# Importance of the tokens in a fused attention and top-k attention kernel: through a row in DRAM instead of through TensorE and ScalarE

## The chip, the core and the metric

The kernel runs on one core of a Trainium2 chip. A core has five engines with instruction queues of their own: TensorE (PE in the profile; its weight loads are PEld), VectorE (DVE), ScalarE (ACT), GpSimd (POOL) and SyncE (SP). Each works through its queue in order. DMAs are issued by SP, ScalarE and GpSimd and are carried out by 16 DMA engines that all of them share. SBUF is the on-chip memory with 128 partitions, PSUM the memory that TensorE writes, in 8 banks.

The metric is the device time of one execution in microseconds, the median of the runs; one more execution is profiled.

## The reference

Two layers work on a batch of 8 images with 512 channels and 32 x 32 = 1024 tokens, in float32. Layer 0 is a GroupNorm and a full self-attention of 8 heads with a residual. Layer 1, which the change is in, is this (cut to what matters):

```python
q, kk, v = (einsum('oc,bcn->bon', w, xf) for w in (wq, wk, wv))
importance = nan_to_num(sum(xf * xf, axis=1), nan=0.0, posinf=0.0, neginf=0.0)
_, idx = top_k(importance, 256)                   # per image
q_sel, k_sel, v_sel = q[:, :, idx], kk[:, :, idx], v[:, :, idx]      # as tokens x channels
q_sel, k_sel = layer_norm(q_sel, ln_w, ln_b), layer_norm(k_sel, ln_w, ln_b)
attn = softmax(clip(q_sel @ k_sel.T * 512 ** -0.5, -80, 80))
out = v with the columns idx replaced by (attn @ v_sel).T
return x + wo @ out
```

The importance of a token is the sum of squares of its 512 channels. The 256 most important tokens of each image attend to each other; all other tokens keep their value.

## The kernel before

**Layer 0** takes most of the time (up to about 1960 us). Its last steps already do the first part of layer 1 for image 0 (b0), `spread_row` and `imp` of b0 included (`importance`, lines 1094 to 1099). What follows about the order of steps is for b1 to b7.

**Layer 1** is cut into small steps, each a function of an image `b` and an index. They follow each other in an order written out by hand: the strings `BATCH` (lines 60 to 72) and `END` (lines 73 to 104). A word is a step's name and index; each `-` behind it means one image earlier, each `+` one image later. `BATCH` is run through once for each image while the steady part lasts, so that in one pass the early steps of one image (`row`, `square`, `finite`, `spread`, `imp`, `count`, `vo`), the middle steps of the image before (`selt`, `qk`, `stats`, `norm`, `score`) and the last steps of the images before that (`att`, `attput`, `fetch`, `back`, `add`) are woven together. `END` does the same for the last images. Inside `tc.manual_schedule` (lines 594 to 605) this order is the order of every engine's queue, SP's too.

For one image the steps that matter here are:

- `row` (lines 245 to 248): TensorE transposes 128 tokens into a PSUM bank; `square` (line 253): ScalarE squares and sums each token's channels, so that `norm[p, j]` is the importance of token `128 j + p`. `keep_row` and `put` copy the tokens and store them to DRAM.
- `finite` (lines 261 to 267): VectorE replaces infinities and NaN and leaves the result in `col`, 128 partitions x 8 columns.
- `spread_row` (lines 269 to 275): TensorE transposes each column of `col`, repeated 128 times, with the identity. The result is that the 1024 importances stand side by side in every partition of two PSUM banks (`pi`). Each call makes four transposes and fills one bank.
- `imp` (lines 277 to 279): ScalarE copies the two banks to SBUF, into `imp`, 128 x 1024. There is one buffer of it.
- `count` (lines 281 to 304): for each of 8 groups of 128 tokens, VectorE compares every token's importance (a scalar of its partition, from `col`) with all 1024 in `imp` and sums up how many are larger, or equal and ahead of it. `place` (lines 329 to 333) adds the counts: this is the token's rank. `pick`, `holder` and `who` make the list of the 256 chosen tokens from the ranks, and `getx` gathers them from DRAM.
- `selt` and `qk`: the chosen tokens are transposed and multiplied with the weights. `stats`, `root` and `norm` (lines 410 to 437) are the LayerNorm on VectorE, with a square root on ScalarE; they end in `rows`. `normt` (line 444) transposes `rows` on TensorE, in two groups of eight matmuls, the first for q, the second for k. `score`, `clip`, `exp`, `probt`, `att` and `attk` are the attention.
- `attput` (line 528): SP stores the attended tokens to DRAM (`sa`). `fetch` (line 534): GpSimd gathers them into their places among the values `V`, 8 gathers for an image. `back` (line 550): TensorE transposes `V` back to channels x tokens (`po`). `add` (line 558): VectorE adds the residual, and SP stores the result and loads a later residual (`residual`, line 544).

PSUM banks are handed out in turn, 8 of them: a new tile waits until the tile eight before it has been read. The weights of layer 1 are loaded once; the images come in with `load_x1` (line 215).

In a pass of `BATCH`, `finite` of image t stands between `back` and `add` steps of earlier images and the `selt` and `qk` steps of image t-1. VectorE's queue after `finite` is: one `add`, five of the eight counts of image t, the LayerNorm of image t-1, then the other counts between later steps. `attput` of image t-2 comes soon after `finite` in the order, ahead of a pair of output store and residual load for each `add`.

Of the kernel before, what the change touches and what calls it, by code (L numbers as in the profile page):

```python
# [9 lines left out]
F32 = mybir.dt.float32  # L10
# [8 lines left out]
P = 128  # L19
B = 8  # L20
C = 512
N = 1024
# [35 lines left out]


BATCH = """  # L60
vkeep6- square1 inv-- put4 put2 holder- add3--- keep1 square2 back4--- att0-- att1-- who-
row6 put1 row0 add4--- row7 keep0 back7--- square0 row3 keep6 attk0-- put0 square3 vo0 row5
vput7- square6 getx- vput4- attk1-- keep3 square7 square5 add7--- vput5- back6--- keep7
finite vo1 attput-- add6--- vput0- vkeep0 keep5 selt1- selt0- spread1 spread0 fetch1-- imp1 imp0
count2 fetch0-- put6 count5 vo3 count7 vkeep1 selk1- selk0- qk1- count6 count3 qk0-
fetch5-- qk2- vput6- vput3- stats0- stats1- vput2- qk3- root0- stats2- root2- fetch2-- norm0-
vkeep3 put5 norm2- vput1- root1- vo4 vkeep4 stats3- fetch3-- norm1- vo2 root3- back0--
fetch6-- fetch4-- norm3- fetch7-- normt1- normt0- count4 vkeep2 add0-- put3 put7 back5--
normt2- normt3- scale2- scale3- row4+ add5-- back1-- scale1- count0 back2-- vo5 scale0-
count1 square4+ keep4+ place score0- score1- clip- back3-- vo6 vkeep5 pick0 add1-- exp- vo7  # L70
getv- add2-- pick1 row2+ probt- vkeep7 row1+ probk- keep2+
"""
END = """
vput2-- put4- vkeep6-- row3- add3---- square2- holder-- att1--- back4---- row0- who-- inv---
put2- row7- square1- keep1- attk1--- att0--- getx-- square3- keep3- keep0- keep7- put1- put3-
put7- row5- back6---- attk0--- row6- square7- back7---- square6- add4---- square0- square5-
keep5- keep6- put0- vput5-- vo1- put5- selt1-- finite- vkeep1- spread1- add6---- add7----
selk1-- selt0-- spread0- imp1- imp0- attput--- count1- vo0- row6 row2 vput7-- selk0-- count6-
keep6 keep2 row1 square2 count0- count2- vput6-- count7- row0 count3- vkeep0- square1 keep1
put1 vput1-- qk0-- row7 qk1-- put6- square0 put2 stats1-- qk3-- stats0-- count5- put6 keep7  # L80
square6 vo7- put7 root1-- vput1- fetch5--- row4 root0-- norm0-- qk2-- keep0 stats3--
fetch3--- count4- vo6- place- square4 vkeep7- keep4 norm1-- square7 root3-- stats2-- row3
vput0- vkeep6- vo4- normt1-- root2-- norm3-- normt0-- vput0-- row5 keep3 fetch1--- vput4--
vput3-- norm2-- vkeep4- scale1-- normt2-- put3 normt3-- scale0-- fetch2--- pick1- scale2--
square5 square3 keep5 put5 vo2- fetch0--- pick0- holder- finite spread0 scale3-- put4 vkeep2-
imp0 getv-- fetch6--- spread1 who- imp1 score0-- back2--- count4 score1-- fetch7--- count2
clip-- exp-- count3 vput2- back0--- count7 getx- vput4- count6 put0 add0--- vo3- count0
fetch4--- probt-- vkeep3- probk-- inv-- add2--- att0-- att1-- attk1-- attk0-- selt1- selt0-
selk1- selk0- attput-- count5 fetch6-- count1 qk3- place stats3- pick0 back3--- back4---
vput6- add4--- root3- pick1 back1--- qk2- fetch4-- qk0- fetch0-- norm3- add3--- fetch2--  # L90
vput7- back7--- stats2- stats0- holder fetch3-- fetch1-- qk1- who vput3- add7--- root0-
root2- add1--- back5--- norm2- getx add5--- back6--- vo5- normt3- stats1- norm0- fetch7--
root1- fetch5-- norm1- normt2- vkeep5- add6--- normt0- normt1- back2-- scale0- scale3-
scale2- back5-- back7-- vput5- add2-- back1-- add1-- selt1 back6-- back3-- scale1- add7--
add5-- score0- add6-- back0-- selt0 score1- selk1 add3-- clip- selk0 qk2 exp- stats2 back4--
qk1 probt- probk- stats1 getv- add0-- qk0 qk3 att1- root2 root1 norm2 norm1 stats0 inv-
stats3 add4-- root0 attk1- vo1 att0- root3 norm3 vkeep1 norm0 attk0- normt3 normt2 normt0
attput- scale3 normt1 fetch5- scale0 scale1 fetch7- fetch6- vo0 vkeep0 scale2 score1 fetch1-
score0 clip vsel1 fetch4- vo3 exp vselk1 vsel0 vselk0 probt fetch0- probk fetch2- vkeep3 vo6
att1 inv fetch3- att0 vo7 vkeep6 vo2 back0- attk1 back2- back4- attk0 vkeep7 back3- attput  # L100
vkeep2 add3- add0- back5- vo4 fetch7 fetch3 vo5 vkeep4 add2- back1- back7- fetch2 back6-
fetch0 fetch1 add4- add1- fetch6 add7- add5- back2 back4 add4 add6- back0 back6 fetch4 vkeep5
add0 fetch5 back3 back7 add2 back1 add6 back5 add3 add7 add1 add5
"""


# [12 lines left out]
def attention_then_topk_attention(  # L119
# [55 lines left out]
    x_dram = [dram.tile([N, C], F32, tag=f"sx{b}", name=f"sx{b}") for b in range(B)]  # L175
    v_dram = [dram.tile([N, C], F32, tag=f"sv{b}", name=f"sv{b}") for b in range(B)]
    a_dram = [dram.tile([TOP, C], F32, tag=f"sa{b}", name=f"sa{b}") for b in range(B)]


    before = const.tile([P, P], F32, tag="before", name="before")  # L180
# [45 lines left out]
    tiles, pools, x1, w = {}, {"r1": keep_pool}, {}, {}  # L226
# [50 lines left out]
    def imp(b, j):  # L277
        t = get("rp", ("imp", b), [P, N], "imp", 1)
        nc.scalar.copy(t[:, ts(j, HALF)], tiles["pi", b, j])

    def count(b, j):

        cnt = get("r1", ("count", b), [P, 3, NB], "count", 2)
        imps = tiles["imp", b]
        mine = tiles["col", b][:, j : j + 1]
        lo, hi = j * P, (j + 1) * P
        junk = tiles.get("junk")
        if junk is None:
            junk = pools["rp"].tile([P, N], F32, tag="junk", name=f"junk_{b}_{j}", bufs=1)
        if lo:  # L290
            nc.vector.tensor_scalar(  # L291
                junk[:, :lo], imps[:, :lo], mine, None, ALU.is_ge, ALU.add,
                accum_out=cnt[:, 0, j : j + 1],
            )
# [260 lines left out]
    def add(b, i):  # L555
# [52 lines left out]
    def layer0():  # L608
        with ExitStack() as st:
# [668 lines left out]
```

## Time and profile before

| | us |
|---|---|
| median of 3 runs | 2457.42 (2457.2 to 2458.29) |
| the profiled execution | 2457.09 |
| its span, from the first to the last instruction | 2455.4 |
| TensorE busy in the span | 2411.7 (98%) |
| VectorE busy | 1950.4 (79%) |
| ScalarE busy | 1405.2 (57%) |
| GpSimd busy | 1162.5 (47%) |
| `b_pi<-ident,col`, line 273, TensorE, x56 | 0.27 each, pipelined |
| `imp<-b_pi`, line 279, ScalarE, x14 | 0.60 each |
| counts, line 297, VectorE, x64 | 0.34 to 1.28 each, by width |
| counts, line 291, VectorE, x56 | 0.34 to 1.15 each, by width |

An instruction of the profile is named by its line, its engine, its operation and `out<-in`, with buffer numbers left out. A matmul's duration overlaps the next one's, so a busy TensorE isn't a TensorE at its peak. In a row of the order of time the first number is the start in us from the span's start, the second the duration; brackets behind a row give the engine's idle time before it and what ended it. `SPq` rows are DMAs being issued by SP. The share of the DMA engines is the mean over the core's 16.

### The profile page before, as it was taken

To read this page: it belongs to the slowest core of one execution; us is meant where nothing else is said; L and a number is where in the kernel's file an instruction comes from. 1 tells how busy PE (TensorE), PEld (TensorE's weight loads), DVE (VectorE), ACT (ScalarE), POOL (GpSimd) and SP (SyncE) were. 2 spreads that over 40 slices of the span, in tenths; PEclk is the share of its full clock that TensorE was granted. 3 is DMA by queue.
4 is the path that set the end of the run, shared out by engine and by line. 5 is a ranking of instruction groups with operands and counts; after the bars stand their busy time and mean duration, and the time that the engine had idled before them with its cause. 6 is when DMAs were issued, how large, how long until landed. Compare 5 with 4: busy or idle time off the path is not lost. (4 is left out here: it accounts for less than half of the span.)

```text
span 2455.4 us, 32009 instructions
## 1 busy us (share of the span) xinstructions
PE 2411.7 (98%) x11724; PEld 969.0 (39%) x11724; DVE 1950.4 (79%) x2946; ACT 1405.2 (57%) x1828; POOL 1162.5 (47%) x557
## 2 busy tenths in 40 slices
PE   7999999999999999999999999999999999999998
PEld 3333333333333333333333333333333345555554
DVE  4899988988898889888988897889877466666683
ACT  2767656665676567666665675567656523333421
POOL 0556645655556456645655555556545401111122
PEclk9999999999999999999999999999999999999999
DMA  3001112111201120112011211111112444567553
GB/s 138 31 31 61 35 57 84 34 44 60 86 32 44 61 78 26 48 57 78 27 56 53 74 44 44 61 40 65 57 56 99 151 140 155 207 204 241 190 192 107
DMA packets 108252, 205.55 MB, mean 84 GB/s; under 512 B 19114, under 2 KB 19370, under 8 KB 108096
## 3 DMA queue, kind: packets, MB, share of 16 engines
q1 hardware_dynamic: 82432, 159.95, 19.4%
q10 hardware_dynamic: 18144, 31.48, 3.4%
q0 software_dynamic: 7520, 12.09, 1.7%
q8 instruction: 92, 1.51, 0.2%
q14 instruction: 64, 0.52, 0.1%
HBM read 146.29 MB, written 69.73 MB: 88 GB/s over the span
## 5 line engine op out<-in xcount | busy, mean ns | idle before, releaser
L1012 POOL TENSOR_TENSOR es<-es,e 128x1024 f32<-128x1024 f32 x384 | 913.4, 2379 | 59.1 <-ACT e L1007 30.9
L953 ACT COPY e<-sc 128x1024 f32<-128x1024 f32 x512 | 510.1, 1009 | 379.5 <-DVE high L959 266.8
L1004 DVE TENSOR_TENSOR e<-e,ns 128x1024 f32<-128x1024 f32 x512 | 594.8, 1215 | 1.2 <-ACT ns L1000 1.1
L1007 ACT ACTIVATE e<-e 128x1024 f32<-128x1024 f32 x512 | 532.0, 1056 | 49.9 <-DVE e L1004 36.4
L1012 POOL TENSOR_TENSOR es<-e,e 128x1024 f32<-128x1024 f32 x64 | 152.6, 2384 | 816.2 <-ACT e L1007 807.1
L945 PE MATMUL sc<-q,k 64*128 64x512 f32 x2048 | 511.0, 617 | 7.2 <-ACT e L953 6.5
L959 DVE TENSOR_TENSOR high<-sc,high 128x1024 f32<-128x1024 f32 x384 | 468.4, 1220 | 43.3 <-PE sc L945 24.5
L1020 PE MATMUL av<-e,v 128*64 128x512 f32 x2048 | 476.0, 596 | 4.5 <-DVE o L1062 4.3
L744 PE MATMUL g<-x,wqkv 128*64 128x512 f32 x1984 | 453.0, 598 | 0.0
L945 PEld LDWEIGHTS sc<-q,k 64*128 64x128 f32 x2048 | 175.7, 186 | 310.6 <-issue 214.4
L1020 PEld LDWEIGHTS av<-e,v 128*64 128x64 f32 x2048 | 144.1, 137 | 303.4 <-issue 285.0
L744 PEld LDWEIGHTS g<-x,wqkv 128*64 128x64 f32 x1984 | 131.4, 136 | 305.9 <-issue 291.3
L744 PE MATMUL g<-wqkv,x 128*64 128x256 f32 x1920 | 220.8, 383 | 0.0
L744 PE MATMUL g<-o,wp 128*64 128x512 f32 x912 | 207.0, 595 | 0.0
L1049 DVE RECIPROCAL rs<-rs 128x256 f32<-128x256 f32 x64 | 112.1, 1752 | 95.8 <-ACT rs L1043 95.8
L744 PEld LDWEIGHTS g<-wqkv,x 128*64 128x64 f32 x1920 | 132.7, 137 | 107.0 <-issue 36.6
L534 POOL DMA_INDIRECT V<-sa,at x64 | 64.0, 1000 | 155.1 <-DMA sa<-att 87.5
L959 DVE TENSOR_TENSOR high<-sc,e 128x1024 f32<-128x1024 f32 x64 | 77.6, 1213 | 52.3 <-ACT e L953 51.7
L744 PEld LDWEIGHTS g<-o,wp 128*64 128x64 f32 x912 | 64.4, 137 | 134.1 <-issue 117.9
L309 PE MATMUL b_pv<-w,x 128*128 128x512 f32 x256 | 115.4, 598 | 0.0
L405 PE MATMUL b_pp<-w,selT 128*128 128x512 f32 x256 | 112.3, 593 | 0.7 <-ACT selT L396 0.7
L363 POOL DMA_INDIRECT sel<-sx,who x16 | 16.1, 1008 | 194.7 <-PE b_po L550 48.4
(177 smaller groups left out, 1990.6 us busy)
## 6 DMA issues: line engine op xcount, KB each, us to landing
nb<-negd SPq DMA_DIRECT2D x128, 256.0 KB, 3.6
x<-in_x_dram SPq DMA_DIRECT2D x32, 512.0 KB, 5.9
ri<-rsd SPq DMA_DIRECT2D x128, 128.0 KB, 2.8
sx<-xT ACTq DMA_DIRECT2D x64, 256.0 KB, 3.2
xr<-in_x_dram SPq DMA_DIRECT2D x58, 256.0 KB, 3.4
x1d<-xr SPq DMA_DIRECT2D x58, 256.0 KB, 4.0
sv<-V ACTq DMA_DIRECT2D x56, 256.0 KB, 3.1
y<-x1d SPq DMA_DIRECT2D x48, 256.0 KB, 4.8
```

Source lines behind the costliest of these rows:

```text
L309: nc.tensor.matmul(pv, x1[b][k][:, ts(j, P)], w["vo"][:, k, :], start=(k == 0), stop=(k == CT - 1),)
L405: nc.tensor.matmul(pp, tiles["selT", b][:, k, ts(rb, P)], w["qk"[which]][:, k, :], start=(k == 0), stop=(k == CT - 1),)
L534: nc.gpsimd.indirect_dma_start(tiles["V", b][:, j, :], None, a_dram[b][:, :], bass.IndirectOffsetOnAxis(ap=tiles["at", b][:, j : j + 1], a ...
L744: nc.tensor.matmul(out[r, :], wide_[:, r], moving, start=(k == 0), stop=(k == CT - 1),)
L945: nc.tensor.matmul(sc[:, hh, :], ks[p][r, ts(j, P)], qs[p][r, ts(hf, HALF)], start=True, stop=True,)
L953: nc.scalar.copy(raw[t, j], banks["s", t, j])
L959: nc.vector.tensor_tensor(high[t], banks["s", t, j], raw[t, 0] if j == 1 else high[t], ALU.max)
L1004: nc.vector.tensor_tensor(raw[t, j], raw[t, j], high[t], ALU.add)
L1007: nc.scalar.activation(raw[t, j], raw[t, j], AF.Exp, scale=QK_SCALE)
L1012: nc.gpsimd.tensor_add(sums[t], raw[t, 0] if j == 1 else sums[t], raw[t, j])
L1020: nc.tensor.matmul(avs[t][HD * hh : HD * hh + HD, :], vs[p // 2][:, j, (p % 2) * P + HD * hh : (p % 2) * P + HD * hh + HD], e[:, hh, :], s ...
L1049: nc.vector.reciprocal(rs[:, : HALF // 2], rs[:, : HALF // 2])
```

## The change

For b1 to b7 the two steps `spread` (twice) and `imp` (twice) are replaced by `nput` and `nget`. `nput` is a DMA issued by SP that stores `col` to a row of 1024 floats in DRAM, `n_dram[b]`, in the order of the tokens: element `[p, a]` of `col` goes to position `128 a + p`. `nget` is a DMA issued by SP that loads this row into each of the 128 partitions of `imp`; it waits for `nput`. Both stand directly behind `finite` in `BATCH` and `END`, and so in SP's queue ahead of `attput` of an earlier image in most passes. The counts read the same `imp` as before. For b0 the end of layer 0 still uses `spread_row` and `imp`. The words of `BATCH` and `END` after this point are the same in the same order, but for the missing ones and for `count1` of b6 in `END`, which moves from ahead of `vo0-` to behind `keep2`, so that VectorE makes count 6 of b6 ahead of count 1.

```diff
 BATCH = """
...
-finite vo1 attput-- add6--- vput0- vkeep0 keep5 selt1- selt0- spread1 spread0 fetch1-- imp1 imp0
-count2 fetch0-- put6 count5 vo3 count7 ...
+... finite nput
+nget vo1 attput-- add6--- vput0- vkeep0 keep5 selt1- selt0- fetch1-- fetch0-- put6 vo3 count2
+count5 count7 ...
...
 END = """
...
-keep5- keep6- put0- vput5-- vo1- put5- selt1-- finite- vkeep1- spread1- add6---- add7----
-selk1-- selt0-- spread0- imp1- imp0- attput--- count1- vo0- row6 row2 vput7-- selk0-- count6-
+keep5- keep6- put0- vput5-- vo1- put5- selt1-- finite- nput- nget- vkeep1- add6---- add7----
+selk1-- selt0-- attput--- vo0- row6 row2 vput7-- selk0-- count6- keep6 keep2 count1- row1
...
-square5 square3 keep5 put5 vo2- fetch0--- pick0- holder- finite spread0 scale3-- put4 vkeep2-
-imp0 getv-- fetch6--- spread1 who- imp1 score0-- back2--- count4 score1-- fetch7--- count2
+pick0- holder- finite nput nget scale3-- put4 vkeep2- getv-- fetch6--- who- score0-- back2---
+count4 score1-- fetch7--- count2 ...
...
+    n_dram = [dram.tile([N], F32, tag=f"sn{b}", name=f"sn{b}") for b in range(B)]
...
+    def nput(b, _):
+        nc.sync.dma_start(n_dram[b].rearrange("(a p) -> p a", p=P), tiles["col", b])
+
+    def nget(b, _):
+
+        nc.sync.dma_start(
+            get("rp", ("imp", b), [P, N], "imp", 1), n_dram[b].unsqueeze(0).to_broadcast([P, N])
+        )
...
     STEPS1 = {
...
-        "spread": spread_row, "imp": imp, "count": count, "vo": vo, "vkeep": vkeep,
+        "nput": nput, "nget": nget, "count": count, "vo": vo, "vkeep": vkeep,
...
-    EARLY = {"row", "square", "keep", "put", "finite", "spread", "imp", "count", "vo", "vkeep", "vput"}
+    EARLY = {"row", "square", "keep", "put", "finite", "nput", "nget", "count", "vo", "vkeep", "vput"}
```

More of the change, by code (lines that the diff above doesn't have):

```diff
@@ L60 @@
 BATCH = """
-vkeep6- square1 inv-- put4 put2 holder- add3--- keep1 square2 back4--- att0-- att1-- who-
-row6 put1 row0 add4--- row7 keep0 back7--- square0 row3 keep6 attk0-- put0 square3 vo0 row5
-vput7- square6 getx- vput4- attk1-- keep3 square7 square5 add7--- vput5- back6--- keep7
-finite vo1 attput-- add6--- vput0- vkeep0 keep5 selt1- selt0- spread1 spread0 fetch1-- imp1 imp0
[L65 to L71, printed above, removed]
+vkeep6- square1 inv-- put4 put2 holder- add3--- keep1 square2 back4--- att0-- att1-- who- row6
+put1 row0 add4--- row7 keep0 back7--- square0 row3 keep6 attk0-- put0 square3 vo0 row5 vput7-
+square6 getx- vput4- attk1-- keep3 square7 square5 add7--- vput5- back6--- keep7 finite nput
+nget vo1 attput-- add6--- vput0- vkeep0 keep5 selt1- selt0- fetch1-- fetch0-- put6 vo3 count2
+count5 count7 vkeep1 selk1- selk0- qk1- count6 count3 qk0- fetch5-- qk2- vput6- vput3- stats0-
+stats1- vput2- qk3- root0- stats2- root2- fetch2-- norm0- vkeep3 put5 norm2- vput1- root1- vo4
+vkeep4 stats3- fetch3-- norm1- vo2 root3- back0-- fetch6-- fetch4-- norm3- fetch7-- normt1-
+normt0- count4 vkeep2 add0-- put3 put7 back5-- normt2- normt3- scale2- scale3- row4+ add5--
+back1-- scale1- count0 back2-- vo5 scale0- count1 square4+ keep4+ place score0- score1- clip-
+back3-- vo6 vkeep5 pick0 add1-- exp- vo7 getv- add2-- pick1 row2+ probt- vkeep7 row1+ probk-
+keep2+
 """
@@ L76 @@
 put7- row5- back6---- attk0--- row6- square7- back7---- square6- add4---- square0- square5-
-keep5- keep6- put0- vput5-- vo1- put5- selt1-- finite- vkeep1- spread1- add6---- add7----
-selk1-- selt0-- spread0- imp1- imp0- attput--- count1- vo0- row6 row2 vput7-- selk0-- count6-
-keep6 keep2 row1 square2 count0- count2- vput6-- count7- row0 count3- vkeep0- square1 keep1
-put1 vput1-- qk0-- row7 qk1-- put6- square0 put2 stats1-- qk3-- stats0-- count5- put6 keep7
-square6 vo7- put7 root1-- vput1- fetch5--- row4 root0-- norm0-- qk2-- keep0 stats3--
@@ L82 @@
-fetch3--- count4- vo6- place- square4 vkeep7- keep4 norm1-- square7 root3-- stats2-- row3
-vput0- vkeep6- vo4- normt1-- root2-- norm3-- normt0-- vput0-- row5 keep3 fetch1--- vput4--
-vput3-- norm2-- vkeep4- scale1-- normt2-- put3 normt3-- scale0-- fetch2--- pick1- scale2--
-square5 square3 keep5 put5 vo2- fetch0--- pick0- holder- finite spread0 scale3-- put4 vkeep2-
-imp0 getv-- fetch6--- spread1 who- imp1 score0-- back2--- count4 score1-- fetch7--- count2
-clip-- exp-- count3 vput2- back0--- count7 getx- vput4- count6 put0 add0--- vo3- count0
@@ L88 @@
[L88 to L103, printed above, removed]
+keep5- keep6- put0- vput5-- vo1- put5- selt1-- finite- nput- nget- vkeep1- add6---- add7----
+selk1-- selt0-- attput--- vo0- row6 row2 vput7-- selk0-- count6- keep6 keep2 count1- row1
@@ new lines @@
+square2 count0- count2- vput6-- count7- row0 count3- vkeep0- square1 keep1 put1 vput1-- qk0--
+row7 qk1-- put6- square0 put2 stats1-- qk3-- stats0-- count5- put6 keep7 square6 vo7- put7
+root1-- vput1- fetch5--- row4 root0-- norm0-- qk2-- keep0 stats3-- fetch3--- count4- vo6- place-
+square4 vkeep7- keep4 norm1-- square7 root3-- stats2-- row3 vput0- vkeep6- vo4- normt1-- root2--
+norm3-- normt0-- vput0-- row5 keep3 fetch1--- vput4-- vput3-- norm2-- vkeep4- scale1-- normt2--
+put3 normt3-- scale0-- fetch2--- pick1- scale2-- square5 square3 keep5 put5 vo2- fetch0---
@@ new lines @@
+pick0- holder- finite nput nget scale3-- put4 vkeep2- getv-- fetch6--- who- score0-- back2---
+count4 score1-- fetch7--- count2 clip-- exp-- count3 vput2- back0--- count7 getx- vput4- count6
+put0 add0--- vo3- count0 fetch4--- probt-- vkeep3- probk-- inv-- add2--- att0-- att1-- attk1--
+attk0-- selt1- selt0- selk1- selk0- attput-- count5 fetch6-- count1 qk3- place stats3- pick0
+back3--- back4--- vput6- add4--- root3- pick1 back1--- qk2- fetch4-- qk0- fetch0-- norm3-
+add3--- fetch2-- vput7- back7--- stats2- stats0- holder fetch3-- fetch1-- qk1- who vput3-
@@ new lines @@
+add7--- root0- root2- add1--- back5--- norm2- getx add5--- back6--- vo5- normt3- stats1- norm0-
+fetch7-- root1- fetch5-- norm1- normt2- vkeep5- add6--- normt0- normt1- back2-- scale0- scale3-
+scale2- back5-- back7-- vput5- add2-- back1-- add1-- selt1 back6-- back3-- scale1- add7-- add5--
+score0- add6-- back0-- selt0 score1- selk1 add3-- clip- selk0 qk2 exp- stats2 back4-- qk1 probt-
+probk- stats1 getv- add0-- qk0 qk3 att1- root2 root1 norm2 norm1 stats0 inv- stats3 add4-- root0
+attk1- vo1 att0- root3 norm3 vkeep1 norm0 attk0- normt3 normt2 normt0 attput- scale3 normt1
@@ new lines @@
+fetch5- scale0 scale1 fetch7- fetch6- vo0 vkeep0 scale2 score1 fetch1- score0 clip vsel1 fetch4-
+vo3 exp vselk1 vsel0 vselk0 probt fetch0- probk fetch2- vkeep3 vo6 att1 inv fetch3- att0 vo7
+vkeep6 vo2 back0- attk1 back2- back4- attk0 vkeep7 back3- attput vkeep2 add3- add0- back5- vo4
+fetch7 fetch3 vo5 vkeep4 add2- back1- back7- fetch2 back6- fetch0 fetch1 add4- add1- fetch6
+add7- add5- back2 back4 add4 add6- back0 back6 fetch4 vkeep5 add0 fetch5 back3 back7 add2 back1
+add6 back5 add3 add7 add1 add5
```

## The prediction

> **What bounds the kernel now.** I read the page's busy shares first, then the busy time by stages, then the waits for `imp`, and last the order of time of VectorE and TensorE around one batch. The profiled execution took 2457.09 us: a span of 2455.4 and 1.69 outside it. The median of the runs, 2457.42, is 0.33 above it; I make the sum against 2457.09 and add 0.33 at the end. Batches are numbered b0 to b7.
>
> The first line is from the page, the others from the busy time by stages (length, then each engine's busy time with its count, TensorE's clock, share of the DMA engines, GB/s).
>
> ```profile
> PE 2411.7 (98%) x11724; PEld 969.0 (39%) x11724; DVE 1950.4 (79%) x2946; ACT 1405.2 (57%) x1828; POOL 1162.5 (47%) x557
> ```
> ```profile
> 2100.00:2150.00 50.00, 49.97 (x184) 27.97 (x184) 31.39 (x99) 19.56 (x44) 11.96 (x12) 1.00 0.65 231
> ...
> 1996.00:2004.00 8.00, 8.00 (x32) 4.54 (x31) 3.90 (x14) 5.42 (x11) 0.03 (x1) 1.00 0.29 100
> ...
> 2114.00:2122.00 8.00, 7.97 (x27) 3.94 (x25) 5.60 (x17) 5.19 (x9) 2.31 (x3) 1.00 1.03 396
> ...
> 2330.00:2338.00 8.00, 8.00 (x54) 5.99 (x53) 6.07 (x20) 3.23 (x5) 4.03 (x5) 1.00 0.55 174
> ```
>
> TensorE has no gap in layer 1's steady part: what leaves its queue is a gain, and what makes it wait is a loss. The three short stages begin where a batch's `col` is finished: the DMA engines are a third busy at b1's, saturated at b3's (0.94 to 1.03 at b3 to b6, 0.74 at b2), half busy at b7's.
>
> How late may `imp` come? VectorE's order after `col` in b3 (start, duration, engine, line; in brackets the idle time and what ended it), then TensorE's.
>
> ```profile
> 2113.93 0.17 DVE L267 SCALAR_TENSOR_TENSOR col<-norm,fin 128x8 f32<-128x8 f32 x1
> ...
> 2116.99 0.48 DVE L291 TENSOR_SCALAR_CACHE_REDUCE junk<-imp,col 128x256 f32<-128x256 f32 x1 [2.25 <-ACT imp L279]
> ...
> 2129.21 0.70 DVE L412 BATCH_NORM_STATS2 lbs<-b_pp 128x6 f32<-128x512 f32 x1 [0.91 <-PE b_pp L405]
> ...
> 2136.80 0.16 DVE L427 RECIPROCAL sd<-sd 128x1 f32<-128x1 f32 x1 [0.41 <-ACT sd L420]
> 2137.77 0.81 DVE L434 TENSOR_SCALAR rows<-b_pp,mv,nt 128x512 f32<-128x512 f32 x1
> ```
> ```profile
> 2139.75 1.04 PE L444 MATMUL b_nt<-ident,rows 128*128 128x128 f32 x8
> 2140.62 0.60 PE L550 MATMUL b_po<-ident,V 128*128 128x128 f32 x4
> 2141.06 1.04 PE L444 MATMUL b_nt<-ident,rows 128*128 128x128 f32 x8
> ```
>
> From the first count (2116.99) to the last normalised rows (2138.58) VectorE needs 21.59 us, 1.32 of it idle: 20.3 of work, five counts and the LayerNorm of the *previous* batch. The second group of `b_nt` (2141.06) transposes those rows. Leaving 0.3 us for the handover and weight load, the first count must start by 2141.06 - 0.3 - 20.3 = 2120.46 for TensorE to be where it is today: 6.36 us after `col` (2114.10). Today it takes 2.89. I call the 6.36 the *break-even delay*.
>
> **The change part by part.**
>
> *Removed from TensorE:* eight transposes a batch, b1 to b7. Between the starts of successive items eight take 0.87 us (2054.60 to 2055.47 at b2), so 7 x 0.87 = 6.1 us. The idle time before them at b4 (1.89, a PSUM bank that ScalarE's `xT` copy frees) stays: the next tile takes the same bank. At b5 (0.89, waiting for `col`) I give half, 0.5, and 0.16 each for the pauses between the two halves at b4 and b5. At most 7 us.
>
> *Removed from ScalarE:* 14 copies of 0.60 us, 8.4. It is 57% busy and its next work, V and selT copies, is not waited for by TensorE for more than 0.43 us anywhere: worth nothing while TensorE has matmuls queued. VectorE's counts are the same; two of them change places in the end order, at no cost.
>
> *Added:* a DRAM round trip between `col` and the first count, and VectorE, which works in order, stands at that count with everything behind it. The trace has the same form in layer 0 (a small store, a wait for it on SP, a broadcast back):
>
> ```profile
> 1917.17 0.37 DVE L985 TENSOR_REDUCE neg<-four 32x32 f32<-32x128 f32 x1
> 1917.57 0.32 SPq L989 DMA_DIRECT2D negd<-neg  x1
> 1918.95 0.81 SPq L994 DMA_DIRECT2D nb<-negd  x2
> ```
> ```profile
> sa<-att SPq DMA_DIRECT2D x1, 512.0 KB, 6.3
> ```
>
> The small store (4 KB in 32 rows) costs 1.38 us from its issue to the issue of the load; issues follow the engine's end by 0.03.
> The new store has 4 KB too, but each of its 1024 four-byte elements lands 512 bytes from the next: 64 pieces on each of 16 DMA engines. The Trainium skill (DMA: Bandwidth & Descriptors, "Rules for kernel authors") says that a last dimension that isn't contiguous becomes one descriptor per element and should be rearranged away: that speaks against this store. Its "Bandwidth" section puts the 64-packet floor at about 10.5 ns a packet; the estimate is then 1.38 + 0.67 = 2.0. From above: q1's packets, nearly all of 2 KB, took on average 0.194 x 16 x 2455.4 / 82432 = 92 ns (the page's queue part); if each element waits a turn behind such a packet, 1.38 + 64 x 0.092 = 7.3. By the row alone the first count would be safe at b3, by the rule not. I take 2.0 (b1), 2.3 (b7), 2.5 (b2) and 3.0 where the engines are saturated, near the lower end since a 4-byte piece moves a five-hundredth of the bytes.
> The load back writes 512 KB. In layer 0 the 256 KB pieces land 3.6 us after issue; the 512 KB `sa` store, issued within 2 us of b3's `col`, took 6.3 (the line above), 6.2 at b5, and 5.1 at b6. I take 4.4 (b1), 5.0 (b7), 5.5 (b2), 6.0 (b3 to b6). With 0.3 for handovers, `col` to first count becomes 6.7, 8.3, four times 9.3, and 7.6 us.
>
> *Break-even delays*, each worked out like b3's from that batch's rows (`col` end; start of the deciding `b_nt` group): b1 1996.55, 2024.36: 7.2. b2 2052.58, 2081.25: 8.1. b4 2175.77, 2204.40: 8.0. b5 2238.11, 2265.07: 6.4. b6 lies in the end order, with 26.1 of work between: 2292.99, 2327.20: 7.8. Delay minus break-even, never below -0.87 (-1.0 at b4, -1.5 at b5): b1 -0.5, b2 +0.2, b3 +2.9, b4 +1.3, b5 +2.9, b6 +1.5; together +8.3. TensorE's saving is in these numbers.
>
> *b7* is different: the end order has no slack.
>
> ```profile
> 2330.05 0.17 DVE L267 SCALAR_TENSOR_TENSOR col<-norm,fin 128x8 f32<-128x8 f32 x1
> ...
> 2333.20 0.74 DVE L291 TENSOR_SCALAR_CACHE_REDUCE junk<-imp,col 128x512 f32<-128x512 f32 x1 [0.38 <-ACT imp L279]
> ```
> ```profile
> 2342.24 3.27 PE L516 MATMUL b_pa<-vs,sT 128*128 128x512 f32 x7 [0.86 <-ACT sT L508]
> ...
> 2370.05 0.98 PE L444 MATMUL b_nt<-ident,rows 128*128 128x128 f32 x7 [0.98 <-DVE rows L434]
> ```
>
> From 2333.20 VectorE runs without idle time to 2372, and TensorE waits twice for what comes out of it: first for the softmax (clip, line 480, stands behind two counts), then for rows. The chain that ended last passes through these counts. So all beyond today's 2.98 us goes to the end: 7.6 - 2.98 = +4.6.
>
> *SP's queue.* At every `col` SP is idle or has just issued its last (b1: nothing between 1990 and 2037; b7: nothing from 2297 to 2345). Behind the new pair stand the previous batch's `attput` and the output stores with their residual loads. At b3 `sa` moves from 2112.05 to about 2117.8, 5.7 later, and the eight `fetch` gathers on GpSimd with it: the last goes out at 2133.9 instead of 2128.2 and lands about 3.9 later, 2137.8, before the `b_po` at 2140.62 that reads it. Margin 2.8; in the slow-store case it is gone, but there the counts are later still. The output stores and residual loads behind it have 25 us of SP idle time (2116 to 2141) to catch up in. Seven loads of 0.52 MB are 3.7 MB of 205.55.
>
> *Sum:* 8.3 + 4.6 = +12.9. 2457.09 + 12.9 = 2470.0; with the 0.33, 2470.3. I say 2470.
>
> **Rivals.**
> A slow store: each 4-byte piece does take a turn behind 2-KB packets (the skill's "Queues, rings and completion order": an engine goes round its queues packet by packet). The store then costs 7.3 at b3 to b6 (+4.3 each) and about 3 more at b2 and b7: +23, 2493. For it: 0.94 to 1.03 in those stages. Against: the trace's 128-byte pieces show no such cost, but in a quiet stage.
>
> The round trip is hidden: it is as short as layer 0's (ScalarE reads `nb` at 1922.45, 4.9 us after `neg`). Below 6.4 us nothing stalls in b1 to b6 and they give 4 x 0.87 + 1.0 + 1.5 = 6.0; b7 still costs 1.9: 2457.4 - 4.1 = 2453.3. It decides where `imp` lands within 6.4 us of `col` in the saturated stages; against it stands 6.3 for `sa` alone.
>
> No change to speak of: delays near 7.5 in b3 to b6 (+1.1, -0.5, +1.1, -0.3), b1 and b2 at -0.5, b7 +3: +3.4, 2461.
>
> **How the numbers follow.** Chances: my forecast (2463 to 2481) 0.50, slow store (2481 to 2510) 0.21, no change to speak of (2453 to 2462) 0.21, hidden and b7 absorbed too (below 2452.5) 0.08. A difference under 0.2%, 4.9 us, can't be told from none here. Slower holds the first two and a sliver of the third, 0.73; same 0.19; faster 0.08. The range, 2454 to 2494, leaves out a tenth at each end; the likeliest case's own is 2463 to 2481.
>
> **What would show it.** In the changed profile: no `b_pi`; the counts' idle time ended by a DMA, 4 us at b1 and 6 at b3; a new idle time of TensorE before `b_nt` of about 1 to 3 us at b3 to b6 and none at b1; before `b_ppt` or `b_pa` in the end order about 4 us more; a median from issue to landing of 2 to 3 us for `sn` and 5 to 6 for `imp`. I am wrong if `sn` lands later than 5 us, if `imp` lands in 4, or if TensorE waits for V (late `fetch`) rather than for rows.

## The result, and the profile after

The changed kernel takes 2527.19 us (median of 4 runs, 2525.61 to 2527.53), beside 2457.86 for the kernel before (4 runs, 2457.2 to 2458.74): 1.0277 times as long, 95% interval 1.0265 to 1.0289, or +69.3 us. I had said 2470, with a range of 2454 to 2494. The sign was right, the size not.

The profiled execution took 2527.3, with a span of 2525.6: 70.2 longer than before. The page's shares, its chain that ended last, and the row of the counts that read `imp` (line 300 is line 291 of before, moved by the diff):

```profile
PE 2424.9 (96%) x11668; PEld 974.6 (39%) x11668; DVE 1947.9 (77%) x2946; ACT 1398.5 (55%) x1814; POOL 1163.5 (46%) x557
...
PE 80%; DVE 8%; DMA 7%; POOL 3%; ACT 2%; issue 1%; ACTq 0%; SPq 0%; DVEq 0%; POOLq 0%
...
L300 DVE TENSOR_SCALAR_CACHE_REDUCE junk<-imp,col 128x128 f32<-128x128 f32 (+6 forms) x56 | 41.6, 743 | 107.0 <-DMA imp<-sn 105.8
```

TensorE's busy time went up by 13.2 us although 56 transposes left it, so it stood idle 57.0 longer; those two make up the 70.2. DMAs are 7% of the chain that ended last. VectorE waited 105.8 us for seven rows, 15.1 each, where I had expected 4 to 6. The waits by engine, TensorE's own (waited for, us in total, times, longest):

```profile
PE b_nt L453 <- DVE rows L443: 20.5, 7, 4.0
PE b_nt L453 <- DVE sd L436: 17.1, 5, 3.9
PE b_ppt L512 <- ACT s L500: 13.9, 1, 13.9
...
PE b_po L559 <- DMA V<-sa,at: 5.5, 5, 1.5
```

Before, TensorE's longest wait for any of these was 1.3. Now 51.5 us are spent in front of the LayerNorm's `rows` and the end order's softmax, both of which stand behind counts on VectorE; 5.5 are for `V`, 2.0 before. So the places are those of the forecast, and what is much longer is the time that leads up to them. The order of time around b3's `col`, first SP, then VectorE, then TensorE:

```profile
2130.73 0.37 SPq L282 DMA_DIRECT2D sn<-col  x1
2141.93 0.32 SPq L286 DMA_DIRECT2D imp<-sn  x1
2142.31 0.43 SPq L537 DMA_DIRECT2D sa<-att  x1
```
```profile
2130.54 0.17 DVE L267 SCALAR_TENSOR_TENSOR col<-norm,fin 128x8 f32<-128x8 f32 x1
...
2146.64 0.48 DVE L300 TENSOR_SCALAR_CACHE_REDUCE junk<-imp,col 128x256 f32<-128x256 f32 x1 [15.30 <-DMA imp<-sn]
```
```profile
2156.66 0.33 PE L559 MATMUL b_po<-ident,V 128*128 128x128 f32 x1 [1.17 <-DMA V<-sa,at]
2160.72 0.45 PE L453 MATMUL b_nt<-ident,rows 128*128 128x128 f32 x1 [3.73 <-DVE sd L436]
2165.01 1.75 PE L453 MATMUL b_nt<-ident,rows 128*128 128x128 f32 x7 [3.85 <-DVE rows L443]
```

The load is issued when the store has completed: 2141.93 - 2130.73 = 11.20 us for 4 KB. From the load's issue to the first count it is 4.7. The store, which I had put at 3.0 here, is the long one. It is so in every pass, and in b1's too, where little else moves:

| | b1 | b2 | b3 | b4 | b5 | b6 | b7 |
|---|---|---|---|---|---|---|---|
| store as predicted | 2.0 | 2.5 | 3.0 | 3.0 | 3.0 | 3.0 | 2.3 |
| store measured, issue to the load's issue | 10.2 | 12.5 | 11.2 | 10.7 | 11.3 | 11.9 | 11.6 |
| `col`'s end to the first count, measured | 14.1 | 17.2 | 15.9 | 15.6 | 15.8 | 16.7 | 16.4 |
| break-even delay of the forecast (b7: today's delay) | 7.2 | 8.1 | 6.4 | 8.0 | 6.4 | 7.8 | 3.0 |
| difference: the loss by the forecast's rule | 6.9 | 9.1 | 9.5 | 7.6 | 9.4 | 8.9 | 13.4 |
| `col` to next `col` (b7: to the end), after minus before | 6.4 | 10.2 | 9.0 | 9.3 | 10.8 | 8.5 | 16.0 |

The fifth line sums to 64.8, the last to 70.2. Put into the forecast's own rule, the measured delays give 92% of the loss. The rule also holds where it says that the loss arises: at b2, b3 and b4 the second group of `b_nt` starts 9.3, 9.7 and 7.7 us later after `col` than before (9.1, 9.5 and 7.6 by the rule). What had to be found out is why a 4-KB store takes 11 us.

### The profile page after: what moved, and what is told of

Its sections match the earlier page's. It is cut to its first block, busy times and chain, and to the rows that moved or that the text cites. A ratio compares the mean times of both kernels' runs of the same rounds, so it can differ in the third digit from the quotient of the medians.

```text
span 2525.6 us, 31897 instructions
## 1 busy us (share of the span) xinstructions
PE 2424.9 (96%) x11668; PEld 974.6 (39%) x11668; DVE 1947.9 (77%) x2946; ACT 1398.5 (55%) x1814; POOL 1163.5 (46%) x557
## 3 DMA queue, kind: packets, MB, share of 16 engines
q10 hardware_dynamic: 18144, 31.48, 4.6%
## 4 chain that ended last, share of the span: by engine, by line
PE 80%; DVE 8%; DMA 7%; POOL 3%; ACT 2%; issue 1%; ACTq 0%; SPq 0%; DVEq 0%; POOLq 0%
PE g L753 32%; PE sc L954 18%; PE av L1029 16%; PE b_pv L318 3%; DMA sn<-col 3%; POOL es L1021 3%; DMA sx<-xT 1%; PE den L1044 1%; DMA imp<-sn 1%; DVE junk L300 1%; PE first L753 1%; PE b_pp L414 1%; PE b_sc L480 1%; DVE junk L306 1%; PE last L753 1%
## 5 line engine op out<-in xcount | busy, mean ns | idle before, releaser
L300 DVE TENSOR_SCALAR_CACHE_REDUCE junk<-imp,col 128x128 f32<-128x128 f32 (+6 forms) x56 | 41.6, 743 | 107.0 <-DMA imp<-sn 105.8
```

Of the source, the lines that this page charges most:

```text
L300: nc.vector.tensor_scalar(junk[:, :lo], imps[:, :lo], mine, None, ALU.is_ge, ALU.add, accum_out=cnt[:, 0, j : j + 1],)
```

## The experiments

My theory was that each 4-byte piece of the store has a fixed price: 10.2 us less the 1.4 of layer 0's small store, over 64 pieces on an engine, is 137 ns. The rivals: the loss comes from what stands behind the pair on SP; any trip through DRAM at this place costs as much; something else in the stage slows the store.

**The round trip without anyone who waits for it.** The kernel before, with the same store behind `finite` and a load of the row (992 of its 1024 values) into a tile that nothing reads. The counts still read what TensorE and ScalarE made.

```diff
+    def ghost(b):
+        nc.sync.dma_start(n_dram[b].rearrange("(a p) -> p a", p=P), tiles["col", b])
+        t = pools["rp"].tile([P, N - 32], F32, tag="ghost", name=f"ghost_{b}", bufs=1)
+        nc.sync.dma_start(t, n_dram[b][: N - 32].unsqueeze(0).to_broadcast([P, N - 32]))
```

> The kernel before, with its transposes and copies, plus the same store of col and a load of the row (992 of its 1024 floats, to save space) into a tile that nobody reads, at the same place in SP's queue: SP's queue is held up and attput and fetch are late, but no count waits. Theory (the counts wait for the row, VectorE stands behind them): 2458 to 2463, since only the three or four waits of TensorE for V of about 1 us each remain. Rival (SP held up for 10 to 12 us at each col makes attput and the fetches late, and this is what costs): more than 2490.

Measured: 2474.92 (2471.49 to 2481.82) beside 2458.47, ratio 1.0079 (1.006 to 1.0097): 16.5 us, between my two numbers and outside both. SP and TensorE at b3 and b4, in the order of time:

```profile
2113.43 0.37 SPq L283 DMA_DIRECT2D sn<-col  x1
2124.13 0.32 SPq L285 DMA_DIRECT2D ghost<-sn  x1
2124.50 0.43 SPq L534 DMA_DIRECT2D sa<-att  x1
```
```profile
2142.89 0.90 PE L556 MATMUL b_po<-ident,V 128*128 128x128 f32 x3 [2.29 <-DMA V<-sa,at]
2207.78 0.55 PE L556 MATMUL b_po<-ident,V 128*128 128x128 f32 x3 [1.48 <-DMA V<-sa,at]
2210.69 0.47 PE L556 MATMUL b_po<-ident,V 128*128 128x128 f32 x1 [2.36 <-DMA V<-sa,at]
```

The store takes 10.7 here too (2113.43 to 2124.13). `attput` stands behind it on SP and goes out at 2124.50, 12.45 after its time of before (2112.05), the gathers with it, and TensorE waits for `V`. From `col` to `col` the four passes b2 to b6 grow by 2.6, 4.6, 3.5 and 2.9, and b7's `col` to the end by 4.0; the stretches ahead of b2's `col` are 3.3 shorter, so that the profiled execution (2471.49, the fastest of the four) is 14.4 longer than before. Of these, TensorE's waits for `V` explain 6.8 (8.8 where they were 2.0); 3.9 us of its waits have no cause that the profile names, and it is busy for 4.6 us longer, most of that at a lower clock (last section). So holding up SP has a cost of its own, which I had missed; most of the changed kernel's 69.3 is still elsewhere.

**`attput` ahead of the pair.** Is that cost part of the 69.3? In the changed kernel one word of `BATCH` is moved, so that SP issues `attput` first at b2 to b5 (b6 and b7 lie in `END`, which stays).

```diff
-... keep7 finite nput
-nget vo1 attput-- add6--- ...
+... keep7 finite attput-- nput
+nget vo1 add6--- ...
```

> The changed kernel, with attput ahead of the pair in the five passes of the steady order (b2 to b6's pair no longer holds it up). Theory: the waits for V (1.17, 0.89, 0.70 us) go, but the rows are late by about 9 us in each pass as before: 2523 to 2527. Rival (late attput): below 2500.

Measured: 2525.94 (2524.15 to 2528.98), ratio 1.0277 (1.026 to 1.0295): no gain, as expected. TensorE's order of time shows where it went:

```profile
2162.39 0.45 PE L453 MATMUL b_nt<-ident,rows 128*128 128x128 f32 x1 [5.71 <-DVE sd L436]
2166.68 1.76 PE L453 MATMUL b_nt<-ident,rows 128*128 128x128 f32 x7 [3.85 <-DVE rows L443]
```

At b3 the 1.17 us for `V` is gone, and the wait for rows right behind it is 5.71 where it was 3.73. The two delays run side by side and the counts' ends last.

**The same bytes in long pieces.** The store writes each partition's 8 values side by side: 128 pieces of 32 bytes. The row then has the tokens in another order, so for b1 to b7 the counts compare with "greater" alone and the mask for equal importances is zero (equal importances would share a rank; what the counts cost does not change).

```diff
-        nc.sync.dma_start(n_dram[b].rearrange("(a p) -> p a", p=P), tiles["col", b])
+        nc.sync.dma_start(n_dram[b].rearrange("(p a) -> p a", p=P), tiles["col", b])
...
-                junk[:, :lo], imps[:, :lo], mine, None, ALU.is_ge, ALU.add,
+                junk[:, :lo], imps[:, :lo], mine, None, ALU.is_ge if in_order_ else ALU.is_gt, ALU.add,
```

> The changed kernel with the row in the order in which col lies in SBUF: 128 pieces of 32 bytes in place of 1024 of 4. The order of the tokens in imp is then another, so the counts of b1 to b7 all compare with greater-than and the tie mask is zero (ties are not broken; the number and the size of the instructions are the same). Theory (the pieces make the store 10 to 12.5 us in place of about 2, and the break-even delays of 6.4 to 8.1 us hold): the delay falls from about 16 to 7 us, b1 to b6 give or take less than 1 each, b7 costs 3.5: 2456 to 2462. Rival (any trip through DRAM at this place costs, the load and the waits included): more than 2480.

Measured: 2469.87 (2468.36 to 2472.25) beside 2458.47, ratio 1.0047 (1.003 to 1.0064), +11.4. 57 of the 69 us are gone with the layout of a 4-KB store. The rest is more than the 2456 to 2462 that I expected, since the delays are not 7 us in every pass. SP, VectorE and TensorE at b3, in the order of time:

```profile
2114.24 0.32 SPq L282 DMA_DIRECT2D sn<-col  x1
2118.31 0.32 SPq L286 DMA_DIRECT2D imp<-sn  x1
```
```profile
2123.85 0.48 DVE L301 TENSOR_SCALAR_CACHE_REDUCE junk<-imp,col 128x256 f32<-128x256 f32 x1 [9.00 <-DMA imp<-sn]
```
```profile
2142.24 1.29 PE L454 MATMUL b_nt<-ident,rows 128*128 128x128 f32 x7 [3.33 <-DVE rows L444]
...
2354.06 1.18 PE L513 MATMUL b_ppt<-ident,s 128*128 128x128 f32 x3 [5.87 <-ACT s L501]
```

The store takes 4.07 here, 2.5 to 4.5 in the others, and the first counts start 7.65, 7.2, 9.6, 9.1, 9.6, 7.1 and 8.45 us after `col`. By the break-even delays that is +0.45 - 0.87 + 3.2 + 1.1 + 3.2 - 0.8 + 5.5 = +11.8. The execution that was profiled took 2472.25, 2.4 above the median; from `col` to `col` its passes grew by 0.0, -0.4, 2.7, 1.3, 5.0 and -0.7, and from b7's `col` to the end by 6.7, together 14.6. So the rule holds to within 2 us in each pass. This kernel is the forecast's case: delays of its size, and its 2470.

**b7 through TensorE again**, first in the changed kernel, then with the long pieces. In `END` the two words `nput nget` of b7 give way to `spread0`, `imp0`, `spread1` and `imp1`, where they were before.

> The changed kernel, with b7 alone through the transposes and copies again. Theory (in the end order all of the delay beyond 2.98 us reaches the end: 16.4 - 3.0 = 13.4): 2512 to 2516. Rival (the end has slack, the loss sits in the steady passes): 2522 or more.

Measured: 2510.27 (2506.29 to 2512.61), ratio 1.0208 (1.0191 to 1.0225), 16.9 less, a little more than I expected. From b7's `col` to the end the changed kernel takes 141.2, this one 127.8: 13.4, as the rule of b7 has it. Of the other 3.5, 2.2 is the difference between executions (the profiled one took 2512.61); 1.3 lies ahead of b7's `col`, where b6's store took 9.9 in place of 11.9 and others vary by as much.

> The store in 128 pieces of 32 bytes (2469.9 us before), and b7's importance through TensorE's transposes and ScalarE's copies again. Theory (b7 has no slack, so that its 8.45 us of delay against 2.98 go to the end, 5.5 us): 2462 to 2466. Rival (b7's loss is an accident of this order): 2468 to 2471.

Measured: 2463.47 (2461.83 to 2466.36), beside 2456.67, ratio 1.0028 (1.0018 to 1.0038). That is 6.4 less than with b7's row in DRAM, or 4.6 when each is set against the kernel before of its own series (+6.8 and +11.4); 5.5 was expected. In the end order the row's delay goes to the end, us for us as far as these runs can tell.

**The store by itself.** The kernel before, with a series of stores on SP in b1's quiet stretch. Each is followed by a small read-back that waits for it, so that a store's time is from its issue to the read-back's.

```diff
+        nc.sync.dma_start(near.rearrange("(a p) -> p a", p=P), col)
+        nc.sync.dma_start(back_, near.rearrange("(p a) -> p a", p=P))
+        nc.sync.dma_start(far.rearrange("(a p s) -> p a s", p=P, s=16)[:, :, 0], col)
+        nc.sync.dma_start(back_[:, 0:1], far.rearrange("(a p s) -> p a s", p=P, s=16)[:, 0:1, 0])
```
(and so on for half, pair and flat)

> The kernel before, with five stores of `col` one after another in b1's quiet stretch, each followed by a read-back that waits for it; the duration of a store is from its issue to the issue of its read-back. Near: 1024 pieces of 4 bytes, written 4 bytes apart from neighbours in other partitions, as the changed kernel does. Far: 1024 pieces of 4 bytes, 64 bytes apart. Half: 512 pieces of 4 bytes. Pair: 512 pieces of 8 bytes. Flat: 128 pieces of 32 bytes. Theory (each piece has a fixed price of about 137 ns on its engine, whatever its size): near 10 us, far 10, half 5.8, pair 5.8, flat 2 to 2.7. Rival (neighbouring writes to one line collide): near 10, far 3 or less. Rival (the bytes set it): half is half of near, pair as long as near. Rival (the stage's traffic sets it): near is well below 10 here, with the DMA engines idle.

SP's order of time:

```profile
1995.66 0.37 SPq L289 DMA_DIRECT2D near<-col  x1
2005.94 0.32 SPq L290 DMA_DIRECT2D back__12517<-near  x1
2006.31 0.43 SPq L291 DMA_DIRECT2D far<-col  x1
2009.31 0.32 SPq L292 DMA_DIRECT2D back__12517<-far  x1
2009.68 0.43 SPq L293 DMA_DIRECT2D half<-col  x1
2017.85 0.32 SPq L294 DMA_DIRECT2D back__12517<-half  x1
2018.22 0.43 SPq L295 DMA_DIRECT2D pair<-col  x1
2023.49 0.32 SPq L298 DMA_DIRECT2D back__12517<-pair  x1
2023.86 0.46 SPq L299 DMA_DIRECT2D flat<-col  x1
2025.98 0.32 SPq L300 DMA_DIRECT2D back__12517<-flat  x1
```

Near 10.28, far 3.00, half 8.17, pair 5.27, flat 2.12. My theory falls: far has the same 1024 four-byte pieces as near and takes 3.0, as the rival of the neighbouring writes had it. Halving the pieces (half) saves a fifth, not half. What near and half have in common is that 16 pieces land in each stretch of 64 bytes; pair has 8, far 1. And for more than half of near's time the DMA engines are hardly at work. Their view for the 10.5 us from 1995.5 to 2006.0 (busy tenths in 40 slices; then queue: packets, MB, share of 16 engines):

```profile
DMA  9592945899510006990000000000100000000000
...
q10 hardware_dynamic: 144, 0.26, 35.0%
q0 software_dynamic: 168, 0.52, 17.7%
q1 hardware_dynamic: 1040, 0.00, 5.6%
```

q1's 1040 packets took 0.056 x 16 x 10.5 = 9.4 us of engine time, 9 ns each, 0.6 us per engine. Taken in windows of a quarter us, they all lie within 3.0 us of the issue, that is before 1998.7; what follows until 2000.2 are packets of other DMAs, from then on the engines record next to nothing, and the completion comes at 2005.9. In half the last piece is moved 1.5 us after the issue, and the completion comes 6.7 us later; in far the two are 2.2 and 0.8. The time isn't in the moving of the pieces but in the wait that follows it, until the store counts as completed.

One rival stays open for the size of these numbers. While near and half were waiting, a 256-KB store of `sx` was issued (3.0 and 3.9 us after them), while far and nearly all of pair had none. Such a store alone doesn't make a small one slow: flat took 2.12 with some 0.4 MB of `sx` moving, and in the whole kernel the long pieces took 2.5 to 4.5 in the same places as the packed ones 10.2 to 12.5. But how long near and half would have waited without it isn't shown.

**The spacing alone.** 1024 pieces of 4 bytes each time, and only their distance changes.

```diff
+        nc.sync.dma_start(two.rearrange("(a p s) -> p a s", p=P, s=2)[:, :, 0], col)
...
+        nc.sync.dma_start(own.rearrange("(p a s) -> p a s", p=P, s=2)[:, :, 0], col)
```

> The kernel before, with six stores of `col` one after another in b1's quiet stretch, 1024 pieces of 4 bytes each, that differ only in how far apart neighbouring partitions' pieces are written: 4, 8, 16, 32 and 64 bytes, and, last, 8 bytes apart with neighbours from the same partition (own). A small read-back waits for each, and the duration is from the issue of the store to that of its read-back. Theory, from the first series (4 bytes apart took 10.3 us, 64 bytes apart 3.0): writes into one stretch of 64 bytes wait for one another, about 0.48 us for each further one. So 10.3, 6.4, 4.5, 3.5 and 3.0, and own 6.4, as 8 pieces share a stretch there too. Rival (only writes of different partitions get in each other's way): own 3.0. Rival (the stretch is 32 bytes): 10.3, 6 to 7, 4 to 4.5, and then 3.0 at 32 and at 64. Rival (the first series' order or its read-backs misled): all about 10.

SP's order of time, the stores at 4, 8 and 64 bytes and the last one:

```profile
1999.20 0.37 SPq L289 DMA_DIRECT2D near<-col  x1
2008.38 0.32 SPq L291 DMA_DIRECT2D back_near<-near  x1
2008.76 0.43 SPq L292 DMA_DIRECT2D two<-col  x1
2013.11 0.32 SPq L294 DMA_DIRECT2D back_two<-two  x1
...
2020.96 0.43 SPq L301 DMA_DIRECT2D sixteen<-col  x1
2023.61 0.32 SPq L303 DMA_DIRECT2D back_sixteen<-sixteen  x1
2023.97 0.60 SPq L304 DMA_DIRECT2D own<-col  x1
2030.14 0.32 SPq L306 DMA_DIRECT2D back_own<-own  x1
```

| distance of neighbouring pieces | 4 B | 8 B | 16 B | 32 B | 64 B | 8 B, same partition |
|---|---|---|---|---|---|---|
| expected | 10.3 | 6.4 | 4.5 | 3.5 | 3.0 | 6.4 |
| measured, us | 9.18 | 4.35 | 3.16 | 3.58 | 2.65 | 6.17 |

The dependence on the distance is there: 4.35, 3.16 and 2.65 at 8, 16 and 64 bytes, with no `sx` store issued meanwhile. It is steeper at the near end than a constant price per further write, though the 9.18 at 4 bytes again had an `sx` store in its wait. So had the 3.58 at 32 bytes, which may be why it is out of order, and the last column had two. Its 6.17 speaks against the rival that only writes of different partitions hinder each other, since at 32 bytes an `sx` store cost tenths, but it doesn't rule it out. How long the stretch is, in which writes wait for one another, these distances do not tell, and each was measured once.

**What the removed work was worth.** The kernel before without its 48 transposes and 12 copies of b2 to b7, with nothing in their place.

```diff
-        imps = tiles["imp", b]
-        mine = tiles["col", b][:, j : j + 1]
+        imps = tiles["imp", min(b, 1)]
+        mine = (tiles["col", b] if b < 2 else tiles["kept"])[:, j : j + 1]
...
+                    if name in ("spread", "imp") and b > 1:
+                        continue
```

> The kernel before without its 48 transposes and 12 copies of b2 to b7: the counts of b2 to b7 read b1's row and a copy of b1's `col`, so that b2 to b7 select b1's tokens, and spreading their importance is left out of the computation. It bounds what the change could have gained with a round trip that costs nothing. Theory (eight transposes are worth 0.87 us a batch, and 1.0 to 1.5 at b4 and b5, ScalarE's copies nothing): 5 to 7 us below the kernel before, 2451 to 2453.5. Rival (the removed work is hidden too): within 2 us of it. Rival (ScalarE's copies held TensorE up): more than 9 us below it.

Measured: 2448.68 (2447.6 to 2450.73) beside 2456.67, ratio 0.9967 (0.9955 to 0.9979): 8.0 us, more than the 5 to 7 that I expected and less than the 9 of the rival, with an interval of 5.2 to 11.1 that reaches both. The trace speaks for the removed matmuls and against ScalarE's copies: TensorE stands idle for 43.8 us in it, as before (43.7), and is busy for 8.7 less (by an estimate 1.7 of that because no wait slowed its clock, see the last section). These 8.0 are all that a round trip for nothing could have gained in these six.

**LayerNorm among the counts.** Long pieces, b7 through TensorE, and in `BATCH` the previous image's `stats`, `root` and `norm` moved up between the counts, so that two counts stand ahead of the first rows instead of five.

```diff
-nget ... vo3 count2
-count5 count7 vkeep1 selk1- selk0- qk1- count6 count3 qk0- fetch5-- qk2- ... stats0-
+nget ... vo3 vkeep1
+selk1- selk0- qk1- qk0- fetch5-- qk2- vput6- vput3- stats1- count2 stats0- ... root1-
+root0- fetch2-- count5 norm0- ... norm1- ... norm2- ... norm3- fetch7-- count7 normt1- ...
```

> The store in 128 pieces of 32 bytes, b7 through TensorE, and in the steady order VectorE's LayerNorm of the previous batch set among the counts, so that less of it stands behind the row. Theory (the rest of the loss is rows that come late because they stand behind the counts): 2454 to 2458, 6 to 10 below the same kernel without the new order. Rival (counts that end later delay the selection instead, or something else is last): no better than 2462.

Measured: 2455.34 (2452.22 to 2459.36) beside 2456.67, ratio 0.9996 (0.9989 to 1.0002); 8.1 below the same kernel in the old order. TensorE's wait for rows goes from 11.8 us in six places to 2.7 in two, of which 1.84 is b6's, in the end order. The new order was not tried on the kernel before by itself; that kernel waits for rows for 1.0 us in all, so this order has little to gain there.

> As the version with the woven order (2455.3 us beside 2456.7 of the kernel before), but with b6's importance through TensorE too, since TensorE still waits 1.84 us for rows after b6's `col` there. Theory: 1.84 less 0.87 for the eight transposes that come back, so about 1 us less than that version, 2453.5 to 2455, and 1.5 to 3 below the kernel before. Rival (the wait is not from the row in DRAM): no better than that version, or 0.9 us worse.

Measured: 2454.66 (2453.2 to 2457.51) beside 2456.22, ratio 0.9995 (0.9987 to 1.0003), and TensorE waits for rows once, for 1.0, as in the kernel before. By the 0.2% this is no difference from the kernel before: with the store in long pieces, the new order, and b6 and b7 through TensorE, the round trip of b1 to b5 through DRAM costs nothing and gains nothing that shows.

## Why the prediction was right and wrong

- *What bounds the kernel* (TensorE without a gap, so that each wait is a loss): right. All but some 3 us of the loss is TensorE waiting, or running slower after a wait.
- *The removed work* (at most 7 us; by 0.87, 1.0 and 1.5 it is 6.0 for b2 to b7): right within the noise, 8.0 (5.2 to 11.1) measured.
- *The break-even delays*, with nothing lost below them and all of it beyond: right. With measured delays they give 64.8 of the span's 70.2 in the changed kernel, and 11.8 with the long pieces, where the medians differ by 11.4 and the profiled execution's passes by 14.6. They leave out what a wait costs after its end (last section).
- *b7 has no slack*: right. 13.4 by rule and 13.4 measured; with the long pieces 5.5 by rule and 4.6 to 6.4 measured.
- *The load*, 4.4 to 6.0: a little high. From its issue to the first count 3.9 (b1), 4.7 (b3), 4.8 (b7); with the long pieces 3.75, 5.5 and 3.9.
- *The store*, "I take 2.0 (b1), 2.3 (b7), 2.5 (b2) and 3.0": this is the step that failed. It took 10.2 to 12.5. Both of its bounds were prices of packets on a DMA engine. The lower one was even right as such: 10.5 ns by the page, 9 in the trace. What it left at the little that layer 0's row holds of it (1.38 with everything) is the time between the last piece and the completion. 1024 pieces packed into one row took 6.5 to 7.3 us longer than as many 64 bytes apart (with a store of `sx` in their wait), and most of that after the last piece had been moved. I had written that each element lands 512 bytes from the next. So it does within a partition; but in the row its neighbour is 4 bytes away and comes from the next partition, and the distance between neighbours is what the stores' times follow. "From above" was no upper bound: 7.3 came from turns behind 2-KB packets, and in the quiet stretch the store takes 9.2 to 10.3 though its pieces have had all their turns after 3.0. The row I had leaned on, 4 KB in 32 rows of 128 bytes at 1.38, was near in bytes and not in what mattered; it is a neighbour of stores in longer pieces (2.1 for 128 of 32 bytes in the quiet stretch).
- *The rule of the Trainium skill* (DMA: Bandwidth & Descriptors, "Rules for kernel authors": a last dimension that isn't contiguous becomes a descriptor per element, rearrange it away) spoke against this store, and I gave it 0.7 us. The runs give the packed layout 6.5 to 7.3, and in the whole kernel 57. The reason stated there, the number of descriptors, isn't what the runs show: with 64 bytes between them as many pieces took 2.65 to 3.0. The page's "Specifications" say that transfers below 512 bytes are done as read-modify-write, and its "Anatomy of one DMA" (of one that GpSimd issues) that a DMA's fixed time is mostly the receipt from the memory written to; both would fit a wait after the last piece. The first alone doesn't tell packed pieces from spaced ones, as both are of 4 bytes. No run here shows the mechanism, only the dependence on distance and the late completion; why neighbouring pieces complete late stays open.
- *SP's queue* ("in the slow-store case it is gone, but there the counts are later still"): right. Moving `attput` gained nothing. But the unread pair costs 16.5 us with no late counts to hide it, which I had not worked out, and my expectation of 2458 to 2463 for the unread row was wrong for that.
- *The rivals*: the slow store (2493, 0.21) was nearest, by its place and not by its cause. The chances went astray with the bound: no case held a store beyond 7.3.
- *The signs named*: "I am wrong if `sn` lands later than 5 us" came in. No `b_pi` of b1 to b7 is left, the counts' wait is ended by a DMA, as said; "none at b1" failed with the store, 1.95 and 3.99 us at b1's pass.

## What to carry to other kernels

A small store isn't over when its last piece has been moved, so bound it by a row that has the same piece size and the same distance between pieces, or measure it; a row with the same number of bytes is no neighbour. Write small results to DRAM in the longest pieces that the source's partitions hold, and let the reader take the order that results, where it doesn't care for the order. When a delay is put ahead of a queue that works in order, compare it with the slack of whatever stands behind it: here that one number per pass, read from two orders of time, held, to within 3 us in a pass, over delays from 7 to 17 us.

## What the runs showed of the hardware

The store's time, above all: 1024 pieces of 4 bytes took 9.2 to 10.3 us when packed, 4.35 at 8 bytes apart, 2.65 to 3.0 at 64 bytes apart, 2.1 as 128 pieces of 32 bytes, in the same quiet stretch, with the DMA engines' own share in the packed one at 0.6 us each.

While a packed store is waiting, other stores are slow too. ScalarE's queue q10 has the same 18144 packets and 31.48 MB in each of these kernels. They take 3.4% of the 16 engines' span before, 3.5% with the long pieces, and 4.6% in the changed kernel: 0.046 x 16 x 2525.6 - 0.034 x 16 x 2455.4 is about 520 us of engine time more, or 4.7 for each store and engine. And the 256-KB store of `sx` that was issued during half landed after 7.0 us, where the median before is 3.2. Why isn't shown.

And TensorE's clock. Stages of the changed kernel around b3's two waits for rows, busy time of each engine with its count, then TensorE's granted clock:

```profile
2150.00:2160.00 10.00, 5.72 (x16) 2.42 (x14) 9.40 (x35) 1.04 (x5) 6.94 (x7) 0.95 0.22 56
2160.00:2165.00 5.00, 0.45 (x1) 0.18 (x1) 4.58 (x17) 1.19 (x4) 1.69 (x2) 0.50 0.42 153
2165.00:2170.00 5.00, 4.99 (x27) 4.99 (x28) 4.79 (x16) 2.07 (x5) 0.31 (x1) 0.57 0.58 170
2170.00:2180.00 10.00, 10.00 (x40) 6.44 (x39) 7.45 (x21) 2.90 (x5) 0.00 (x0) 1.00 0.33 100
```

Two waits of 3.7 and 3.85 us took the clock to 0.50, and in the 5 us after them, with TensorE busy again, it was still 0.57: seven `b_nt` take 1.75 there, eight took 1.04 before. The Trainium skill (TensorE: Matmul & The Clock Gate, "Part 1") says much the same: half the clock after an idle window of about 3.4 us, and full again after as long a busy one. But a shorter wait can be enough. In the kernel before, b4's wait of 1.89 us was followed by a clock of 0.50 from about 2176.5 to 2179.9:

```profile
2175.91 1.66 PE L273 MATMUL b_pi<-ident,col 128*128 128x128 f32 x8 [1.89 <-ACT xT L256]
```

Eight of these take 1.04 at b2. The wait of 1.84 before b6's `b_nt` in the woven order left the clock at 1.00. I had counted a wait at its length; one of about 2 us or more can cost slow matmuls besides. In half-us stretches from 1960 us on, TensorE works for 36.7 us at a clock below 0.9 in the changed kernel and for 3.5 before. My estimate from the clock in each stretch is 17.7 and 1.7 us lost by it, 16 more. Less some 6 us for the 56 transposes that left, that accounts for 10 of the 13.2 us that TensorE is busy longer; the rest stays open.
